# Filler products on TensorE between the attention steps of the last two groups

## The chip, the cores and the metric

The kernel runs on one core of a Trainium2 chip. The metric is the device time of one execution in microseconds (us): 2128.97 us before the change, the median of three runs (2126.75 to 2130.69). The profile is of one execution with a span of 2129.0 us, so its positions can be read against that number. Engines are named as in the profile: PE is TensorE's matrix product, PEld its weight load, DVE is VectorE, ACT is ScalarE, POOL is GpSimd, and SP issues the transfers.

## What is computed

There are 128 graphs of 128 nodes with 256 features each. Two residual layers follow one another, both on a normalised and rectified input:

```python
h = maximum(layernorm(x), 0)
x = x + gated_graph_network(h, adj, ...)      # three GRU layers
h = maximum(layernorm(x), 0)
x = x + attention(h, adj, W)

# attention
Wh = h @ W
s = Wh.sum(-1)
e = leaky_relu(s[:, :, None] + s[:, None, :], 0.2)
e = where(adj == 0, -inf, e)
alpha = softmax(e, -1)
out = alpha @ Wh
```

Everything is in float32. The change lies in the second layer, the attention, and in the layer norm ahead of it.

## The kernel before

The 128 graphs are cut into 32 groups of four (`G = 4`, `NG = 32`). Each group passes through three GRU layers and then through the attention. The work of several groups overlaps: while one group does its GRU products, earlier groups do their attention between them. At the end of the kernel this ends too. The last two groups, 30 and 31, have their attention when few or no GRU products are left, and group 31 is cut into two halves (graphs 2 and 3 first, then 0 and 1) so that one half can work while the other waits.

The order of the instructions is not that of the code. Each step calls `op(engine, ns, fn, reads, writes, ...)`, which only records a node: the engine, a cost in nanoseconds written by hand, and what it depends on. `Plan.run` then plays a schedule with these costs. It picks the engine whose earliest possible start comes first, and on this engine, among the nodes that can start at that time, the one of lowest rank. A node's rank is its due time, or that of what depends on it less the costs in between, whichever is earlier. The instructions are emitted in the order found, and each engine works them off in that order, waiting for semaphores where it must. Costs in the code are thus guesses that set the order; the chip takes the time that it takes. GRU products form a chain of fixed order.

A buffer tag has a number of instances and a kind. A write of a new instance depends on all accesses of the earlier instance that it replaces. Instances of kind "turn" are handed on in the order of their phase. `h1` has one instance, `top` and `low` two, `st`, `mv`, `rs` and `nm` eight. In PSUM there is one bank each for `x_rz`, `x_n`, `y_rz`, `y_n`, `q_rz`, `q_n`, which belong to the GRU products, and two banks `misc` for everything else.

The attention of a group, with the lines that the prediction uses:

- `normed(x1, h1)`: statistics of each graph on DVE (`st`, L488), their aggregation (`mv`, L493), the reciprocal root on POOL (`rs`, L497 and L498), a small product (`nm`, L500), and the normalised, rectified `h1` on ACT (L504).
- `hw` and `s` (L899): the row sums that the scores are made of, on DVE.
- `turn_s` (L923): four or two transposes of `s` on PE. L929, L930 and L932 make the scores `e` on DVE; L934 takes their maximum `top`, L936 makes `low` of it.
- `exps` (L941) on ACT. L943 and L944 make the sums and their reciprocals.
- In the last two groups, transposes of `e` on PE (L953) and a copy to `eT` on ACT (L955).
- `weighted` (L619): two sets of products of `h1` and `eT` on PE, each followed by a copy to `uT` on ACT (L624).
- `rows_product` (L966): the product with `W`, in two sets for four graphs. L971 on DVE scales it and adds the residual, L974 stores the result.

The GRU products of the last layer are L670. At the very start, L309 fills two banks with products of the identity matrix by itself, and L344 is a transpose of weights.

Of the kernel before, what the change touches and what calls it, by code (L numbers as in the profile page):

```python
# [36 lines left out]
class Plan:  # L37
# [25 lines left out]
        uses.append(b)  # L63
        return b

    def op(self, eng, ns, fn, reads=(), writes=(), room=(), due=None, mark=None,
           turn=None, two=False, lag=None):

        i, deps = len(self.nodes), set()
        for b in room:
            if b.prev is not None:
                deps.update(a[0] for a in b.prev.accesses)
        for is_write, group in ((False, reads), (True, writes)):
            for item in group:
                b, lo, hi = item if isinstance(item, tuple) else (item, 0, 1 << 30)
                for j, w, l, h in b.accesses:
                    if (w or is_write) and l < hi and lo < h:  # L80
                        deps.add(j)
                if is_write and b.prev is not None:
                    deps.update(a[0] for a in b.prev.accesses)
        for is_write, group in ((False, reads), (True, writes)):
            for item in group:
                b, lo, hi = item if isinstance(item, tuple) else (item, 0, 1 << 30)
                b.accesses.append((i, is_write, lo, hi))
        deps.discard(i)
        bufs = {id(x[0] if isinstance(x, tuple) else x): (x[0] if isinstance(x, tuple) else x)
                for x in list(reads) + list(writes) + list(room)}  # L90
        free = [b for b in bufs.values() if self.tags[b.tag][1] in ("free", "turn")]
        for b in free:
            b.users.append(i)
            b.left += 1
        self.nodes.append([eng, ns, fn, deps, free, self.due if due is None else due,
                           two or eng == "POOL", self.LAG[eng] if lag is None else lag])
        if due is not None:
            self.chain.append(i)
        if mark is not None:
            self.marks[mark] = i  # L100
        if turn is not None:
            self.turns.append((i, turn))
# [108 lines left out]
def kernel(  # L211
# [79 lines left out]
    def ap(b):  # L291
        return phys[(b.tag,) + b.slot]
# [187 lines left out]
        to_sbuf("ACT", D, ps, W["w1_sum"], 0)  # L480


    def normed(src, dst, lo=0, hi=G):

        st, mv, rs, nm = buf("st"), buf("mv"), buf("rs"), buf("nm")
        part = slice(lo, hi)
        for b in range(lo, hi):
            op("DVE", 415, lambda b=b: nc.vector.bn_stats(ap(st)[:, b, :], ap(src)[:, b, :]),  # L488
               [(src, b, b + 1)], [(st, b, b + 1)])

        def aggr():
            for b in range(lo, hi):
                nc.vector.bn_aggr(ap(mv)[:, b, :], ap(st)[:, b, :])  # L493
        op("DVE", 160 * (hi - lo), aggr, [st], [mv])

        def rstd():
            nc.gpsimd.tensor_tensor(ap(rs)[:, part], ap(mv)[:, part, 1], eps[:, part], OP.add)  # L497
            nc.gpsimd.tensor_tensor(ap(rs)[:, part], ap(rs)[:, part], neghalf[:, part], OP.pow)  # L498
        op("POOL", 1300, rstd, [mv], [rs])
        op("DVE", 170, lambda: nc.vector.scalar_tensor_tensor(  # L500
            ap(nm)[:, part], ap(mv)[:, part, 0], -1.0, ap(rs)[:, part], op0=OP.mult, op1=OP.mult),
           [mv, rs], [nm])
        for b in range(lo, hi):
            op("ACT", 520, lambda b=b: nc.scalar.activation(  # L504
                ap(dst)[:, b, :], ap(src)[:, b, :], AF.Relu, bias=ap(nm)[:, b:b + 1],
                scale=ap(rs)[:, b:b + 1]), [(src, b, b + 1), rs, nm], [(dst, b, b + 1)])

    def flat(b):
        return ap(b).rearrange("p q n -> p (q n)")
# [381 lines left out]
    def attention(g, a, x1, h1, lo, hi):  # L891

        part, n = slice(lo, hi), hi - lo
        w1, w1_sum = W["w1"], W["w1_sum"]
        normed(x1, h1, lo, hi)
        s = buf("s")
        for b in range(lo, hi):
            hw = buf("hw")
            op("DVE", 520, lambda b=b, hw=hw: nc.vector.scalar_tensor_tensor(  # L899
                ap(hw), ap(h1)[:, b, :], 1.0, ap(w1_sum), op0=OP.mult, op1=OP.mult,  # L900
                accum_out=ap(s)[:, b:b + 1]), [(h1, b, b + 1), w1_sum], [hw, (s, b, b + 1)],
               two=True)

        e, top, low, den, rden = (buf(t) for t in ("e", "top", "low", "den", "rden"))

        def wide(t):
            return ap(t)[:, part, None].to_broadcast([P, n, N])

        def es():
            return ap(e)[:, part]

        def small(t):
            return ap(t)[:, part]
        cost = 155 + 134 * n
        op("DVE", 150 + 66 * n, lambda: nc.vector.tensor_scalar(
            es(), ap(a)[:, part], 0.0, -BIG, op0=OP.is_equal, op1=OP.mult), [(a, lo, hi)], [e])
        s_all = buf("misc")

        def turn_s():
            for b in range(lo, hi):
                nc.tensor.transpose(flat(s_all)[:, b * N:(b + 1) * N],  # L923
                                    ap(s)[:, b:b + 1].to_broadcast([P, P]), ident)

        def spread():
            return flat(s_all)[:, lo * N:hi * N].rearrange("p (b n) -> p b n", n=N)
        op("PE", 110 * n, turn_s, [s], [s_all], [e])
        op("DVE", cost, lambda: nc.vector.tensor_tensor(es(), es(), spread(), OP.add), [s_all], [e])  # L929
        op("DVE", cost, lambda: nc.vector.tensor_tensor(es(), es(), wide(s), OP.add), [s], [e],  # L930
           two=True)
        op("DVE", cost, lambda: nc.vector.scalar_tensor_tensor(  # L932
            es(), es(), ALPHA, es(), op0=OP.mult, op1=OP.max), [], [e], two=True)
        op("DVE", cost, lambda: nc.vector.tensor_reduce(small(top), es(), AX.X, OP.max),  # L934
           [e], [top])
        op("DVE", 150, lambda: nc.vector.tensor_scalar(  # L936
            small(low), small(top), -BIG / 1e3, -1.0, op0=OP.max, op1=OP.mult), [top], [low])

        def exps():
            for b in range(lo, hi):  # L940
                nc.scalar.activation(ap(e)[:, b, :], ap(e)[:, b, :], AF.Exp, bias=ap(low)[:, b:b + 1])  # L941
        op("ACT", 320 * n, exps, [low], [e], turn=(g + 2, 1, "rz"))
        op("DVE", cost, lambda: nc.vector.tensor_reduce(small(den), es(), AX.X, OP.add), [e], [den])  # L943
        op("DVE", 170, lambda: nc.vector.reciprocal(small(rden), small(den)), [den], [rden])  # L944
        eT, uT = buf("eT"), buf("uT")
        if g < NG - 2:
            turned_weights(e, eT)
        else:
            p_e = buf("misc")

            def turn():
                for b in range(lo, hi):
                    nc.tensor.transpose(flat(p_e)[:, b * N:(b + 1) * N], ap(e)[:, b, :], ident)  # L953
            op("PE", 110 * n, turn, [e], [p_e], [eT])
            op("ACT", 190 + 100 * n, lambda: nc.scalar.copy(  # L955
                ap(eT)[:, part].rearrange("p b n -> p (b n)"), flat(p_e)[:, lo * N:hi * N]),
               [p_e], [(eT, lo, hi)])

        weighted(h1, eT, uT, lo, hi)
        for m in range(lo, hi, 2):  # L960
            ps = buf("misc")

            def rows_product(m=m, ps=ps):
                for b in range(2):
                    for k in range(KD):
                        nc.tensor.matmul(ap(ps)[:, b, :], ap(uT)[:, k, (m + b) * N:(m + b + 1) * N],  # L966
                                         ap(w1)[:, k, :], start=(k == 0), stop=(k == KD - 1))
            op("PE", 4 * 432, rows_product,
               [(uT, m // 2, m // 2 + 1), (uT, 2 + m // 2, 3 + m // 2), w1], [ps])
            for b in range(2):  # L970
                op("DVE", 480, lambda b=b, i=m + b, ps=ps: nc.vector.scalar_tensor_tensor(  # L971
                    ap(x1)[:, i, :], ap(ps)[:, b, :], ap(rden)[:, i:i + 1], ap(x1)[:, i, :],
                    op0=OP.mult, op1=OP.add), [ps, rden], [(x1, m + b, m + b + 1)])
        op("SP", 100, lambda: nc.sync.dma_start(  # L974
            out[g * G + lo:g * G + hi].rearrange("b n d -> n b d"), ap(x1)[:, part]),
           [(x1, lo, hi)], [])
# [49 lines left out]
```

## Time and profile before

| stage, us from the start | what PE does | granted clock |
|---|---|---|
| 2080 to 2090.67 | last GRU products (L670), transposes L923 of group 30 | 1.00 |
| 2090.67 to 2094.40 | L966 of group 29 | 1.00 |
| 2094.40 to 2097.00 | nothing | 0.96 |
| 2097 to 2111 | attention of group 30 | 0.52 |
| 2111 to 2114 | little: transposes L923 of group 31 | 0.97 |
| 2114 to 2121 | attention of group 31 | 0.52 |
| 2121 to 2125 | rest of group 31 | 1.00 |
| 2125 to 2129 | nothing: last L971 and the last store | 0.81 |

A stage's clock is the mean share of full TensorE speed that was granted. The profile has several views that are used below: the page with each engine's busy share and the clock in 40 slices, the chain of waits (the steps that ended last, each released by the one before it), the busy time of each engine in chosen stages, and the instructions in order of time. A count xN there is a count of instructions, not of products in the code. PE durations are modelled and overlap; the starts of the weight loads (PEld) show better how fast consecutive products run.

### The profile page before, as it was taken

How to read it: one execution, taken by the hardware profiler on the slowest of the kernel's cores; microseconds unless marked ns; L12 is line 12 of the kernel's file. 1: busy time of each engine (PE TensorE's matmuls, PEld its weight loads, DVE VectorE, ACT ScalarE, POOL GpSimd, SP SyncE). 2: the span in 40 equal slices, each digit the busy share in tenths (PEclk: the TensorE clock that was granted, in tenths of full speed). 3: DMA queues.
4: the chain of work that ended last, by engine and by line, in shares of the span. 5: the costliest groups of instructions: out<-in, count | busy, mean ns of one | idle time of the engine just before them, and what ended most of it. 6: DMA issues, size and time to landing. Idle time of an engine off the chain costs nothing. (4 is left out here: it accounts for less than half of the span.)

```text
span 2129.0 us, 34073 instructions
## 1 busy us (share of the span) xinstructions
PE 2108.4 (99%) x12550; PEld 1882.8 (88%) x12550; DVE 1701.3 (80%) x3364; ACT 1536.5 (72%) x2771; POOL 923.8 (43%) x889
## 2 busy tenths in 40 slices
PE   8999999999999999999999999999999999999997
PEld 7888888898888998889998898998889988898896
DVE  7767898778787887877888787887878887877785
ACT  5567787767777676877767777677776777676663
POOL 5544454344543435434444443444434454434331
PEclk9999999999999999999999999999999999999997
DMA  4222223232222322323222322222223222212220
GB/s 144 45 50 50 48 51 72 50 65 54 64 67 55 79 56 50 68 58 80 45 60 58 75 67 50 65 56 64 66 55 75 60 50 70 60 31 53 58 75 30
DMA packets 333430, 129.35 MB, mean 61 GB/s; under 512 B 264656, under 2 KB 333008, under 8 KB 333264
## 3 DMA queue, kind: packets, MB, share of 16 engines
q1 hardware_dynamic: 333264, 127.18, 26.3%
q8 instruction: 98, 1.61, 0.3%
q14 instruction: 68, 0.56, 0.1%
HBM read 45.36 MB, written 16.78 MB: 29 GB/s over the span
## 5 line engine op out<-in xcount | busy, mean ns | idle before, releaser
L702 ACT COPY t_rz<-y_rz 128x512 f32<-128x512 f32 x192 | 112.3, 585 | 188.8 <-PE y_rz L663 114.3
L565 POOL TENSOR_TENSOR r<-rows 128x512 f32<-128x512 f32 x128 | 140.4, 1117 | 229.8 <-ACT rows L548 99.9
L712 DVE TENSOR_TENSOR t_rz<-t_rz,q_rz 128x512 f32<-128x512 f32 x192 | 131.3, 684 | 88.0 <-PE q_rz L663 40.4
L633 POOL TENSOR_TENSOR hs<-hT 128x512 f32<-128x512 f32 x96 | 131.8, 1373 | 156.3 <-PE y_n L670 72.4
L663 PE MATMUL y_rz<-hs,s_hh 128*128 128x256 f32 x768 | 197.4, 379 | 0.3 <-ACT t_rz L702 0.3
L663 PE MATMUL y_rz<-gs,s_x 128*128 128x256 f32 x768 | 197.1, 379 | 0.0
L663 PEld LDWEIGHTS y_rz<-gs,s_x 128*128 128x128 f32 x768 | 145.9, 190 | 19.8
L637 POOL TENSOR_TENSOR hs<-hT,hs 128x256 f32<-128x256 f32 x96 | 77.0, 802 | 198.1 <-PE q_n L670 160.4
L663 PEld LDWEIGHTS y_rz<-hs,s_hh 128*128 128x128 f32 x768 | 144.0, 190 | 20.1 <-issue 1.0
L590 POOL TENSOR_TENSOR pl<-d,pl 128x512 bf16<-128x512 f32 x64 | 80.8, 1264 | 185.1 <-ACT pl L588 184.9
L568 POOL TENSOR_TENSOR p<-r 128x512 bf16<-128x512 f32 x128 | 159.6, 1267 | 0.0
L712 DVE TENSOR_TENSOR t_n<-t_n,q_n 128x512 f32<-128x512 f32 x192 | 131.3, 684 | 26.4 <-PE q_n L670 12.6
L585 POOL TENSOR_TENSOR d<-hT,pl 128x512 f32<-128x512 f32 x64 | 77.6, 1214 | 139.2 <-DVE hT L791 65.2
L608 ACT COPY aT<-misc 128x512 f32<-128x512 f32 x192 | 112.0, 585 | 27.1 <-PE misc L605 23.3
L663 PE MATMUL x_rz<-hT,s_hh 128*128 128x256 f32 x512 | 131.5, 379 | 0.0
L663 PE MATMUL x_rz<-aT,s_x 128*128 128x256 f32 x512 | 131.4, 379 | 0.0
L966 PE MATMUL misc<-w,uT 128*128 128x256 f32 x512 | 125.5, 390 | 0.8 <-ACT uT L624 0.7
L829 POOL TENSOR_TENSOR x<-x,u 128x512 f32<-128x512 f32 x64 | 82.5, 1305 | 100.1 <-DMA x<-in_x_dram 54.9
L785 DVE TENSOR_TENSOR d<-hT,u 128x512 f32<-128x512 f32 x128 | 115.4, 901 | 10.5 <-ACT u L782 10.5
L663 PE MATMUL y_n<-hs,s_hh 128*128 128x256 f32 x384 | 114.3, 379 | 0.0
L663 PE MATMUL y_n<-gs,s_x 128*128 128x256 f32 x384 | 114.3, 379 | 0.0
L966 PEld LDWEIGHTS misc<-w,uT 128*128 128x128 f32 x512 | 98.6, 196 | 15.6 <-ACT uT L624 2.1
(219 smaller groups left out, 6418.5 us busy)
## 6 DMA issues: line engine op xcount, KB each, us to landing
rows<-in_x_dram SPq DMA_DIRECT2D x32, 512.0 KB, 4.2
x<-in_x_dram SPq DMA_DIRECT2D x32, 512.0 KB, 4.0
out_dram<-x SPq DMA_DIRECT2D x31, 512.0 KB, 2.9
at<-in_adj_dram SPq DMA_DIRECT2D x32, 256.0 KB, 2.8
plT<-pl SPq DMA_TRANSPOSE x186, 3.3
rz<-in_L_gnn_w_ih_dram SPq DMA_DIRECT2D x1, 768.0 KB, 5.0
rz<-in_L_gnn_w_hh_dram SPq DMA_DIRECT2D x1, 768.0 KB, 7.7
e<-in_L_gnn_weight_dram SPq DMA_DIRECT2D x3, 256.0 KB, 7.8
```

Source lines behind the costliest of these rows:

```text
L565: op("POOL", 1106, lambda part=part: nc.gpsimd.tensor_tensor(ap(r1)[:, part], ap(rows)[:, part], top(rows)[:, part], OP.subtract), [(rows, ...
L568: op("POOL", 1050, lambda part=part: nc.gpsimd.tensor_tensor(ap(p3)[:, part], ap(r1)[:, part], top(r1)[:, part], OP.subtract), [(r1, n, n ...
L585: op("POOL", 1150, lambda k=k, r=r: nc.gpsimd.tensor_tensor(ap(r), ap(hT)[:, k], part(pl, k, 0), OP.subtract), [(hT, 2 * k, 2 * k + 2), (p ...
L590: op("POOL", 1150, lambda k=k, r=r: nc.gpsimd.tensor_tensor(part(pl, k, 2), ap(r), part(pl, k, 1), OP.subtract), [r], [(pl, k, k + 1)])
L608: op("ACT", 590, lambda k=k, ps=ps: nc.scalar.copy(ap(dst)[:, k, :], flat(ps)), [ps], [(dst, 2 * k, 2 * k + 2)])
L633: op(eng, cost, lambda: sub(ap(w)[:, 0:2, :], blocks()[:, 1::2, :], blocks()[:, 0:2, :], OP.subtract), [t], [(w, 0, 2)], two=True)
L663: nc.tensor.matmul(ap(bank)[:, half, :], ap(w)[:, i - 1, q, :], source(t, sums), start=(first and c == 0 and m == 0), stop=False, skip_gro ...
L702: op("ACT", 590, lambda: nc.scalar.copy(ap(t), ap(y)), [y], [t], mark=mark)
L712: op("DVE", 690, lambda: nc.vector.tensor_tensor(ap(t), ap(t), ap(q), OP.add), [q], [t])
L785: op("DVE", 690, lambda j=j, d=d, cols=cols: nc.vector.tensor_tensor(ap(d), ap(hT)[:, j, :], ap(u)[:, cols], OP.subtract), [(hT, lo, hi), ...
L829: op("POOL", 1290, lambda cols=cols, part=part: nc.gpsimd.tensor_tensor(part(x1), part(x1), ap(u)[:, cols], OP.add), [(u, lo, hi)], [(x1, ...
L966: nc.tensor.matmul(ap(ps)[:, b, :], ap(uT)[:, k, (m + b) * N:(m + b + 1) * N], ap(w1)[:, k, :], start=(k == 0), stop=(k == KD - 1))
```

## The change

A helper `warm(t, ns, get)` is added. It acts only in the last two groups. It records one more PE node with a planned cost of `60 + ns`: one product of the identity matrix with a small part of `t`, the result of a step that has just been recorded, and `ns // 110` products of the identity with itself. All of them accumulate into the bank `x_n`, which nobody reads any more. A filler therefore can't start before the step's result is there, nor before the last GRU step has read `x_n`. It is meant to keep PE busy while the attention's short steps run on the other engines, so that the clock is not lowered. The nodes get a due time of 10^9, so that they are taken after any real work that can start at the same time, unless something real depends on them.

Fillers are added after each graph's statistics (330), after `mv` (1100), after `nm` (440), after each graph's `h1` (440), after `top` (110) and after `low` (330 for each graph). Group 30 gets them for four graphs at once, group 31 for two graphs in each half.

```diff
-    def op(self, eng, ns, fn, reads=(), writes=(), room=(), due=None, mark=None,
+    def op(self, eng, ns, fn, reads=(), writes=(), room=(), due=None, mark=None, late=False,
            turn=None, two=False, lag=None):
...
-        self.nodes.append([eng, ns, fn, deps, free, self.due if due is None else due,
+        self.nodes.append([eng, ns, fn, deps, free, 10 ** 9 if late else self.due if due is None else due,
...
+    def warm(t, ns, get=None):
+        if plan.group < NG - 2:
+            return
+        if not after_gates:
+            phase_now, plan.phase = plan.phase, len(turns)
+            after_gates.append(buf("x_n"))
+            plan.phase = phase_now
+        b = after_gates[0]
+        def products():
+            here = flat(b)
+            what = get() if get else plain(t)[:, :P]
+            cols = what.shape[1]
+            nc.tensor.matmul(here[:, :cols], ident, what, start=False, stop=False, skip_group_check=True)
+            for _ in range(ns // 110):
+                nc.tensor.matmul(here[:, :P], ident, ident, start=False, stop=False,
+                                 skip_group_check=True)
+        op("PE", 60 + ns, products, [t, b], [], late=True)
+    after_gates = []
...
+            if dst is not src:
+                warm((st, b, b + 1), 330, lambda b=b: ap(st)[:, b, :])
...
+        if dst is not src:
+            warm(mv, 1100, lambda: ap(mv)[:, lo, :])
...
+        if dst is not src:
+            warm(nm, 440, lambda: ap(nm)[:, part])
...
         for b in range(lo, hi):
+            warm((h1, b, b + 1), 440, lambda b=b: ap(h1)[:, b, :P])
...
+        warm(top, 110, lambda: small(top))
...
+        warm(low, 330 * n, lambda: small(low))
```

## The prediction

> **What bounds the kernel now.** I read the page's shares and clock row first, then the chain of waits, then engine totals by stage over the last 41 us, then the weight loads of the same stretch in order of time. Page:
>
> ```profile
> PE 2108.4 (99%) x12550; PEld 1882.8 (88%) x12550; DVE 1701.3 (80%) x3364; ACT 1536.5 (72%) x2771; POOL 923.8 (43%) x889
> PEclk9999999999999999999999999999999999999997
> ```
>
> TensorE is busy nearly throughout, so every product added costs time unless it falls into an idle stretch. Only the last slice has a low clock. By stages:
>
> ```profile
> 2088.00:2090.67 2.67, 2.67 (x19) 2.44 (x18) 1.85 (x4) 0.93 (x2) 1.06 (x1) 1.00 0.01 3
> 2090.67:2094.40 3.73, 3.73 (x19) 2.97 (x17) 3.62 (x8) 0.91 (x2) 0.22 (x1) 1.00 0.00 0
> 2094.40:2097.00 2.60, 0.00 (x0) 0.00 (x0) 2.60 (x5) 0.89 (x4) 1.57 (x1) 0.96 0.00 0
> 2097.00:2111.00 14.00, 11.92 (x38) 9.55 (x38) 9.21 (x30) 4.28 (x9) 2.21 (x4) 0.52 0.11 37
> 2111.00:2114.00 3.00, 0.70 (x6) 0.22 (x4) 2.56 (x8) 0.46 (x2) 0.00 (x0) 0.97 0.00 0
> 2114.00:2121.00 7.00, 6.50 (x20) 5.10 (x21) 2.68 (x9) 2.31 (x7) 0.00 (x0) 0.52 0.22 75
> 2121.00:2125.00 4.00, 3.33 (x17) 2.21 (x15) 0.91 (x3) 0.74 (x2) 0.00 (x0) 1.00 0.19 66
> ```
>
> Columns are stage, length, busy us (and count) of PE, weight load, DVE, ACT and POOL, clock, DMA share, GB/s. TensorE does its last gate product until 2090.67, group 29's L966 until 2094.40, then idles 2.60 us; the next stage has clock 0.52. A second gap brings it to 0.52 again. The chain of waits goes through the slow products:
>
> ```profile
> 2098.82 2.09 PE misc L619 x8
> 2104.32 6.72 PE misc L966 x16
> 2117.76 3.42 PE misc L966 x8
> 2124.97 0.48 DVE x L971
> ```
>
> So the change aims at a real loss. Weight loads pace consecutive products; their rows give the full and half rates:
>
> ```profile
> 2077.97 0.97 PEld L619 LDWEIGHTS misc<-eT,h 128*128 128x128 f32 x8
> 2078.86 0.73 PEld L670 LDWEIGHTS y_rz<-s_hh,hs 128*128 128x128 f32 x4
> 2090.67 3.33 PEld L966 LDWEIGHTS misc<-w,uT 128*128 128x128 f32 x16
> 2098.81 1.78 PEld L619 LDWEIGHTS misc<-eT,h 128*128 128x128 f32 x8 [1.08 <-ACT eT L955]
> 1.36 1.78 PEld L309 LDWEIGHTS y_rz<-ident 128*128 128x128 f32 x8 [1.36 <-POOL ident masks.py:199]
> 3.02 1.64 PEld L309 LDWEIGHTS y_n<-ident 128*128 128x128 f32 x8
> 6.05 0.36 PEld L344 LDWEIGHTS x_rz<-ident,rz 128*128 128x128 f32 x3
> 6.37 0.36 PEld L344 LDWEIGHTS misc<-ident,rz 128*128 128x128 f32 x3
> ```
>
> L619 makes 4 float32 products of 128 columns per buffer and shows x8: **two instructions a product**. At full clock 8 of them take 2078.86-2077.97 = 0.89 us, 111 ns each, so 222 ns a product; at half clock 1.78/8 = 222 ns each. L309 is `matmul(ident, ident)`, the filler's own operation: 4 products a tile, again x8, 8 in 3.02-1.36 = 1.66 us, the half rate. Only a transpose (L344, three in 6.37-6.05 = 0.32 us) takes one instruction of 107 ns. L966's 256-column products take about 3.43 us for 16 instructions, 214 ns each.
>
> **What the Trainium skill says.** "FP8 and Floating Point Precision", TensorE Precision Notes: true FP32 goes through the array in four passes. The trace agrees: 222 ns is four times 55. "TensorE: Matmul & The Clock Gate", Part 1: the clock falls to half after an idle window of about 3.4 us and comes back after a busy one. The trace agrees on both levels (1.00 and 0.50); here a gap of 2.60 us sufficed. The same page, Part 3, what overlaps: matrix products start and end strictly in program order. The trace agrees: group 31's first L923 had its operand at 2105.77 (end of L899's second accumulator read) and ran only at 2110.67, behind the last of L966. So whatever stands behind a filler waits for all of it.
>
> **The change, part by part.** Nothing is removed. All work before about 2087.5 keeps its order, because every filler needs tile x_n, whose last reader, L815, ends at 2087.47, and TensorE is busy with gates until 2090.67.
>
> Count: a filler has 1 + ns//110 products. Group 30 (n = 4): st 4x(1+3) = 16, mv 1+10 = 11, nm 1+4 = 5, h1 4x(1+4) = 20, top 2, low 1+12 = 13: 67. Each half of group 31 (n = 2): 8+11+5+10+2+7 = 43. Together **153 products, 306 instructions**. At 111 ns that is **34.0 us** of TensorE at full clock. The planner charges 60+ns: 6.77 us for group 30 and 4.33 us for each half, 15.4 us in all. It takes a product for 110 ns, which the L344 rows show to be a transpose's price; it is half of what L309 and L619 cost.
>
> Room: the real products after 2090.67, at full clock: L966 three times 3.43 (groups 29, 30 and the two halves of 31) = 10.3, L619 32 x 0.111 = 3.55, transposes L953 and L923 16 x 0.135 = 2.16 less the four of group 30's L923, which ran earlier, = 1.62. Sum 15.5 us. From 2090.67 to the last real product's end, 2124.94, are 34.3 us, so 18.8 us of idle and half-clock time are there for fillers. By planned cost (15.4) they fit; by measured cost (34.0) they overrun by 15 us.
>
> Gain inside that sum: half-clock time returns. L619 of group 30 saves 2x0.89, its L966 about 2.9, group 31's L619 0.9, L966 about 1.3: some 7 us. I have counted it by pricing everything at full clock.
>
> Where they land: the planner takes whichever ready instruction starts first, and the lowest rank among equals. The four h1 fillers of group 30 inherit a due time, because group 31 overwrites h1 (one buffer), so they are not really late; I expect them ahead of group 29's L966. Then 4x1.11 = 4.4 us go before it; L971 on VectorE, which started at 2096.05, has to wait until about 2097.1 for the first half and 2098.8 for the second, with L832, L835 and the statistics of group 31 queued behind it: about 2 us on VectorE. Group 30's low filler (13 products, 2.9 us) goes ahead of its transposes L953, and behind them wait eT, L619, uT and L966. Between the two L619, and before each later step, more fillers stand than the gap has room for. Having been ready long before, they never wait themselves, so TensorE just runs on.
>
> Sum, assuming no idle TensorE after 2090.67 and all but two small top fillers (0.9 us) ahead of the last L966: 2090.67 + 15.5 + 33.1 = 2139.3 for its end. After it come L971 and the store, 2129.0-2124.94 = 4.06 us, as before: **2143.4**. If fillers stood last instead, TensorE alone would still run to 2140.1, so no order rescues it.
>
> Costs without a row: 20 leading products move only 2 to 6 columns. Each still loads 128 weight columns, so at most 222 ns; at least nothing. The low end takes 20x0.22 = 4.4 us off: 2139. I take the full price, since loads and products alternate at equal cost in L619. The semaphore waits of the 28 fillers cost nothing where their result is long there; at 0.05 us each (the pieces named issue in the chain of waits are 0.02 to 0.04 us) they are 1.4 us more. Buffer turnover in misc (two banks) or the longer chain through ACT could still idle TensorE for a few us: to 2150.
>
> **The rivals.** (1) **Fillers as cheap as planned**: 153x0.110 = 16.8 us fit into 18.8, the 7 us come back, and some five overruns of half a filler (0.3 us) are lost: 2129-7+1.5 = about 2123, faster. For it: the gaps and clock losses are real. Against it: x8 on L309 and L619. (2) **Partly hidden**: the small products free and half a dozen fillers behind the last L966, or gain and cost near balance: 2129 to 2138. Against it: even then 306 instructions have to finish. (3) **The clock does not stay up on identity data**, or the longer chain opens new gaps: 33 us of fillers at half rate would add far more, 2155 and up. Against it: the L309 products, made of nothing but identity, last 421 ns at the median and 274 ns at the least, so identity data had raised the clock before their row ended.
>
> **How the numbers follow.** Main case, 2138 to 2150: 0.78; (1) 0.08; (2) 0.08; (3) 0.06. Predicted 2143. The range takes in the free small products and some of (2) below, new stalls above: 2135 to 2151. Faster by over 0.2% (under 2124.7): 0.08; within: 0.03; slower: 0.89.
>
> **What would show it.** Right: weight loads of L309's kind under the new line, x306 in all, near 111 ns apart; clock 1.00 from 2090 to the end; no TensorE gap over 1 us there; first L971 after 2096 delayed; the last L966 ending near 2139. Wrong: one instruction a product, a gap left unfilled, or clock at 0.5 while fillers run.

## The result, and the profile after

With the fillers the kernel takes **2145.43 us** (median of four runs, 2145.34 to 2145.6) against 2129.24 us for the kernel before in the same comparison: 1.0077 times as long, 95% interval 1.006 to 1.0095, or some 16 us more. The clock was held as intended, and the kernel is slower all the same.

The page of the kernel after, shares, clock by slices, and the first line of the chain of waits:

```profile
PE 2130.9 (99%) x12856; PEld 1910.1 (89%) x12856; DVE 1700.8 (79%) x3364; ACT 1537.0 (72%) x2771; POOL 924.5 (43%) x889
...
PEclk9999999999999999999999999999999999999999
...
PE 98%; DVE 1%; DMA 1%; ACT 0%; issue 0%; POOL 0%; SPq 0%; DVEq 0%; POOLq 0%
```

The count of PE instructions has risen from 12550 to 12856, by **306**. The last slice's clock is up from 7 to 9 (tenths of full speed). The chain of waits of the kernel before broke off near 2096, in the waits between engines; now it runs along PE alone, back through the whole kernel, since TensorE never waits for anybody in the last stretch. Busy time by stages, columns as in the view of before:

```profile
2090.67:2094.40 3.73, 3.73 (x36) 3.73 (x35) 3.66 (x8) 0.63 (x1) 0.67 (x1) 1.00 0.00 0
2094.40:2097.00 2.60, 2.60 (x14) 2.32 (x14) 1.56 (x3) 1.28 (x4) 0.91 (x1) 1.00 0.00 0
2097.00:2111.00 14.00, 14.00 (x123) 13.87 (x123) 7.87 (x24) 3.06 (x6) 2.21 (x4) 1.00 0.11 39
2111.00:2125.00 14.00, 14.00 (x113) 13.53 (x112) 6.99 (x24) 2.54 (x7) 0.00 (x0) 1.00 0.12 39
2125.00:2139.00 14.00, 14.00 (x115) 13.64 (x114) 0.88 (x2) 1.86 (x5) 0.00 (x0) 1.00 0.06 20
```

TensorE is busy in all of every stage and the clock is 1.00 in all of them (0.80 from 2139 to the end, where no real product is slowed by it). DVE, which was busy 9.21 us from 2097 to 2111, is busy 7.87 there and 0.88 in the last stage, where it now waits for TensorE. The weight loads in order of time (start, length, line, tiles, count) say what it is doing. L499 is the leading product of a filler, L501 the identity products, L649 and L999 are the old L619 and L966 (the line numbers shift a little from kernel to kernel below):

```profile
2089.87 0.30 PEld L499 LDWEIGHTS x_n<-h,ident 128*128 128x128 f32 x2
2090.09 0.97 PEld L501 LDWEIGHTS x_n<-ident 128*128 128x128 f32 x8
...
2094.34 3.33 PEld L999 LDWEIGHTS misc<-w,uT 128*128 128x128 f32 x16
...
2098.01 2.76 PEld L501 LDWEIGHTS x_n<-ident 128*128 128x128 f32 x24
...
2137.56 1.60 PEld L999 LDWEIGHTS misc<-w,uT 128*128 128x128 f32 x8
```

Four products of the identity show x8, twelve x24. A leading product takes 2090.09-2089.87 = 0.22 us. The four h1 fillers of group 30 run from 2089.87 to 2094.34, 4.47 us, ahead of group 29's last product. The last real product ends its loads at 2139.16. VectorE's step behind group 29's L999 (L1004 is the old L971) now waits for it:

```profile
2096.38 0.87 DVE L1004 SCALAR_TENSOR_TENSOR x<-misc,rden,x 128x256 f32<-128x256 f32 x2 [1.04 <-PE misc L999]
```

Where did the 16 us go? From the end of the last gate product's loads to the end of the span it was 2129.0-2090.67 = 38.3 us before and is 2143.7-2089.87 = 53.8 us after. This stretch, called **the tail** below, is 15.5 us longer, nearly the whole difference of the medians. What comes ahead of it varies by a few us between profiles (it ended at 2089.87 in this one and at 2092.84 in one below), so profiles are compared by their tails and kernels by their medians.

### The profile page after: what moved, and what is told of

Its sections match the earlier page's. It is cut to its first block, busy times and chain, and to the rows that moved or that the text cites. A ratio compares the mean times of both kernels' runs of the same rounds, so it can differ in the third digit from the quotient of the medians.

```text
span 2143.7 us, 34689 instructions
## 1 busy us (share of the span) xinstructions
PE 2130.9 (99%) x12856; PEld 1910.1 (89%) x12856; DVE 1700.8 (79%) x3364; ACT 1537.0 (72%) x2771; POOL 924.5 (43%) x889
## 3 DMA queue, kind: packets, MB, share of 16 engines
q8 instruction: 101, 1.65, 0.3%
## 4 chain that ended last, share of the span: by engine, by line
PE 98%; DVE 1%; DMA 1%; ACT 0%; issue 0%; POOL 0%; SPq 0%; DVEq 0%; POOLq 0%
PE y_rz L693 15%; PE q_rz L693 10%; PE x_rz L693 10%; PE y_rz L700 8%; PE y_n L693 8%; PE misc L635 6%; PE q_rz L700 5%; PE x_n L693 5%; PE x_rz L700 5%; PE q_n L693 5%; PE misc L999 5%; PE y_n L700 4%; PE x_n L700 3%; PE q_n L700 3%; PE misc L649 3%; PE x_n L501 1%
## 5 line engine op out<-in xcount | busy, mean ns | idle before, releaser
L999 PE MATMUL misc<-w,uT 128*128 128x256 f32 x512 | 120.6, 380 | 0.0
L693 PEld LDWEIGHTS x_rz<-aT,s_x 128*128 128x128 f32 x512 | 97.2, 190 | 13.2
```

Of the source, the lines that this page charges most:

```text
L693: nc.tensor.matmul(ap(bank)[:, half, :], ap(w)[:, i - 1, q, :], source(t, sums), start=(first and c == 0 and m == 0), stop=False, skip_gro ...
```

## The experiments

**The theory** is the sum: after the last gate product TensorE has 15.5 us of real work at full clock, the fillers, and 4.1 us follow the last real product. As long as TensorE has no idle time in between, the tail is the sum of the three, and each product of 128 columns costs 222 ns wherever it stands. **The rivals**: the loss comes from a few places where a filler stands right ahead of a product on the chain (place); it comes only from the price that the planner was told (price); and the clock is worth nothing here, so that any filler is a loss (clock).

| kernel | fillers, us | sum, us | tail measured, us | median, us | ratio to before, 95% interval |
|---|---|---|---|---|---|
| before | 0 | | 38.3 (clock lost) | 2129.24 | |
| after | 34.0 | 53.6 | 53.8 | 2145.43 | 1.0077 (1.006 to 1.0095) |
| half the products | 18.9 | 38.5 | 38.6 | 2131.52 | 1.0009 (1.0001 to 1.0018) |
| transposes | 20.0 | 39.6 | 38.6 | 2131.06 | 1.0007 (0.9999 to 1.0016) |
| no h1 fillers in group 30 | 29.5 | 49.1 | 51.0 | 2143.78 | 1.0069 (1.0054 to 1.0084) |
| no mv fillers in group 31 | 29.1 | 48.7 | 49.3 | 2142.44 | 1.0062 (1.0047 to 1.0077) |
| identity products in bfloat16 | 13.2 | 32.8 | 33.3 | 2125.93 | 0.9984 (0.9977 to 0.9991) |
| leading products only | 6.2 | 25.8 | 37.2 (clock lost) | 2129.57 | 1.0002 (0.9993 to 1.001) |
| all bfloat16, no h1 in 30 | 7.4 | 27.0 | 32.7 | 2125.38 | 0.9981 (0.9974 to 0.9988) |
| the same, filled to plan | 12.2 | 31.8 | 33.5 | 2126.09 | 0.9985 (0.9978 to 0.9992) |
| true price in the plan | 34.0 | (see below) | 50.6 | 2143.24 | 1.0066 (1.005 to 1.0083) |
| unpaced | 7.4 | 27.0 | 33.0 | 2126.25 | 0.9986 (0.9979 to 0.9992) |

Fillers are products times 222 ns (float32), 110 ns (transpose) or 56 ns (bfloat16); the tail is that of the one profiled run of each kernel. The kernel before ran beside all of these with medians of 2129.2 to 2129.8 us.

**Half the products.**

```diff
-            for _ in range(ns // 110):
+            for _ in range(ns // 220):
```

> Same 28 fillers in the same order with the same planned costs, but ns // 220 instead of ns // 110 identity products: 85 products instead of 153. Sum theory (TensorE has no idle time after 2090, so every product costs its 222 ns): 68 x 0.222 = 15.1 us less than the changed kernel, 2130.3, or 1 to 2 us more where a filler is now too short for its gap; clock near 1.00. Place theory (the loss comes from the few fillers right ahead of a real product on the chain): about half of the loss stays, 2137. A third, that the clock is worth nothing here: 2134 or more.

Measured: 2131.52 us. 68 products fewer took 13.9 us off the median and 15.2 off the tail, 223 ns a product; TensorE is without idle time to the last product and the clock 1.00. This fits the sum, not the place theory's 2137 nor the clock theory's 2134 or more. The kernel is slower than before by some 0.1%: what the clock gives back, these fillers take.

**Transposes in place of the identity products.**

```diff
-                nc.tensor.matmul(here[:, :P], ident, ident, start=False, stop=False,
-                                 skip_group_check=True)
+                nc.tensor.transpose(here[:, :P], ident, ident)
```

> Each identity-by-identity product becomes a transpose of the identity (one instruction of 107 to 135 ns instead of two of 111 ns); the 28 leading products stay. Fillers then take 28 x 0.222 + 125 x 0.107 to 0.135 = 19.6 to 23.1 us. Sum theory: 10.9 to 14.4 us less than the changed kernel, 2131 to 2134.5, clock 1.00. Rival (transposes do not count as activity for the clock, as the Trainium skill says in TensorE: Matmul & The Clock Gate, Part 4): the clock falls to 0.5 in the stretches of transposes, real products are slow again, 2138 or more.

Measured: 2131.06 us, tail 38.6 us, at the fast end. The first stage of the tail, all filler transposes in one row (count, shortest, median and longest load in ns; the loads overlap), and three rows in order of time:

```profile
2090.60:2100.00 9.40, 9.40 (x74) 8.99 (x73) 9.03 (x17) 2.83 (x7) 1.80 (x2) 1.00 0.00 0
...
L501 PEld LDWEIGHTS x_n<-ident x125: 139/141/227, 2090.8 to 2122.9; 128*128 128x128 f32 x125
...
2108.66 1.16 PEld L501 LDWEIGHTS x_n<-ident 128*128 128x128 f32 x10
2109.79 0.30 PEld L499 LDWEIGHTS x_n<-nm,ident 128*128 128x128 f32 x2
2109.93 0.50 PEld L501 LDWEIGHTS x_n<-ident 128*128 128x128 f32 x4
```

125 instructions stand where 250 did before, and ten of them start within 2109.79-2108.66 = 1.13 us, so the planner's 110 ns is about the price of a transpose, and with it the same list of fillers in the same order is 14 us faster. The tail is 1.0 us shorter than the sum: by the starts of their loads the fillers took 19.0 us, since the small leading products take 0.14 us here instead of 0.22. The clock stays at 1.00 though some two thirds of the fillers' time is transposes. The Trainium skill ("TensorE: Matmul & The Clock Gate", Part 4) says that they do not count as activity in the same way; here they kept the clock up. From 2108.66 to 2111.94 products that are not transposes took only 0.58 us of 3.28, less than the share after which the clock fell with leading products only (below). A tail of transposes alone was not tried.

**Leave out 20 products at the most exposed place, or 22 elsewhere.**

The first kernel has no h1 fillers in group 30:

```diff
-            warm((h1, b, b + 1), 440, lambda b=b: ap(h1)[:, b, :P])
+            if g == NG - 1:
+                warm((h1, b, b + 1), 440, lambda b=b: ap(h1)[:, b, :P])
```

The second has no mv fillers in group 31:

```diff
-            warm(mv, 1100, lambda: ap(mv)[:, lo, :])
+            if plan.group == NG - 2:
+                warm(mv, 1100, lambda: ap(mv)[:, lo, :])
```

> Leaves out only group 30's four h1 fillers, 20 products that run ahead of group 29's last product L966 and hold VectorE behind it. Sum theory: 20 x 0.222 = 4.4 us less than the changed kernel, 2141.0, although VectorE's steps now come about 2 us earlier. Place theory: these four carry most of the loss, 2136 or less.

> Leaves out only group 31's two mv fillers, 22 products that stand in other places, in no one's way by the plan. Sum theory: 22 x 0.222 = 4.9 us less than the changed kernel, 2140.5. Place theory: they fill real gaps, nothing changes, 2145.

Measured: 2143.78 and 2142.44 us; tails 51.0 and 49.3 us, 2.8 and 4.5 us shorter than after the change. The place theory had the first as the large gain and the second as none; the less exposed fillers brought more. In medians the gains are 1.7 and 3.0 us, short of the 4.4 and 4.9 that the sum had forecast (2141.0 and 2140.5). In the first profile the stretch ahead of the tail is 1.0 us longer (until 2090.90) than after the change; in the second, of a run of 2143.84 us, it is 3.0 us longer, and TensorE idles for 0.48 us. The first tail falls 1.6 us short of the sum, and its weight loads show why (L987 is the old L953, L1000 the old L966):

```profile
2131.57 0.20 PEld L987 LDWEIGHTS misc<-ident,e 128*128 128x128 f32 x2 [0.21 <-ACT uT L654]
2132.01 1.59 PEld L1000 LDWEIGHTS misc<-w,uT 128*128 128x128 f32 x8 [0.25 <-ACT uT L654]
...
2134.97 0.52 PEld L649 LDWEIGHTS misc<-eT,h 128*128 128x128 f32 x4 [0.71 <-ACT uT L654]
...
2136.20 1.16 PEld L1000 LDWEIGHTS misc<-w,uT 128*128 128x128 f32 x6 [0.48 <-ACT uT L654]
```

The brackets are idle time: 0.21+0.25+0.71+0.48 = 1.65 us. The planner had used the remaining fillers earlier, none was left for the last gaps, and TensorE waited for ACT there. 4.4 less 1.65 is the 2.8 us measured.

**The identity products in bfloat16.** `ident16` is a bfloat16 copy of the identity.

```diff
-                nc.tensor.matmul(here[:, :P], ident, ident, start=False, stop=False,
+                nc.tensor.matmul(here[:, :P], ident16, ident16, start=False, stop=False,
```

> The identity-by-identity products are made in bfloat16 ([...]56 ns apart in the rows of L605 in the kernel before); the 28 leading products stay float32; order and planned costs as in the change. Fillers take 28 x 0.222 + 125 x 0.056 = 13.2 us, which fits into the 18.8 us of room. Sum theory: from the last gate product to the end 15.5 + 13.2 + 4.1 = 32.8 us plus the idle time that remains, against 38.3 before: faster than before by 3 to 5.5 us, 2124 to 2127, clock near 1.00. Rival (the clock is worth nothing, fillers only cost): no faster than before, 2129.8 or more. Rival (cheap products leave gaps and the clock falls all the same): 2129 to 2131.

Measured: 2125.93 us, **faster than before** by 3.2 us (interval 0.9977 to 0.9991), tail 33.3 us with 0.7 us idle. Group 30's product with `W`, before (L966) and here (L1001), and a filler's bfloat16 products:

```profile
2104.32 6.32 PEld L966 LDWEIGHTS misc<-w,uT 128*128 128x128 f32 x16 [0.97 <-ACT uT L624]
...
2102.60 3.32 PEld L1001 LDWEIGHTS misc<-w,uT 128*128 128x128 f32 x16 [0.49 <-DVE x L1006]
...
2106.41 0.65 PEld L503 LDWEIGHTS <-ident 128*128 128x128 bf16 x10
2107.02 0.30 PEld L501 LDWEIGHTS x_n<-nm,ident 128*128 128x128 f32 x2
```

The real product runs at full rate, and ten bfloat16 products take 0.61 us. Fillers of the same number, order and place, 125 of the 153 at a quarter of the price, turn the loss into a gain. The rival that the clock is worth nothing falls here. The kernel before bears this out without any filler: in one of the 57 runs that stood beside this kernel its granted clock was 0.999, and it took 2124.94 us; the other 56, at 0.995 to 0.998, took 2127.32 us or more.

**Leading products only, against all fillers in bfloat16.**

```diff
             nc.tensor.matmul(here[:, :cols], ident, what, start=False, stop=False, skip_group_check=True)
-            for _ in range(ns // 110):
-                nc.tensor.matmul(here[:, :P], ident, ident, start=False, stop=False,
-                                 skip_group_check=True)
```

> Only the 28 leading products (6.2 us), same order and planned costs. Real products and fillers are 21.7 us of the 34.3 us up to the last product, so TensorE must idle. If such short pulses hold the clock: 2122 to 2125. If the clock falls in the gaps as before: 2128 to 2130, since the gap of 2.6 us before the first L953 is filled by 0.2 us only.

```diff
-            nc.tensor.matmul(here[:, :cols], ident, what, start=False, stop=False, skip_group_check=True)
+            nc.tensor.matmul(here[:, :cols], ident16, what.bitcast(BF16).rearrange("p (c two) -> p c two", two=2)[:, :, 1], start=False, stop=False,
+                             skip_group_check=True)
...
-                nc.tensor.matmul(here[:, :P], ident, ident, start=False, stop=False,
+                nc.tensor.matmul(here[:, :P], ident16, ident16, start=False, stop=False,
...
-            warm((h1, b, b + 1), 440, lambda b=b: ap(h1)[:, b, :P])
+            if g == NG - 1:
+                warm((h1, b, b + 1), 440, lambda b=b: ap(h1)[:, b, :P])
```

> All filler products in bfloat16, the leading ones too (they take the upper halves of the step's result), and group 30's h1 fillers left out, so that nothing stands ahead of group 29's L966. 133 x 0.056 = 7.4 us of fillers, half of what the planner thinks. Sum theory with the clock held: floor 15.5 + 7.4 + 4.1 = 27 us, so waits on other engines set the end, 2122 to 2124. If too little filling lets the clock fall: 2126 to 2129.

Measured: 2129.57 and 2125.38 us. The second lies between its two expectations: the clock held, but 2122 to 2124 was too low. The two have nearly the same amount of fillers, 6.2 and 7.4 us, and differ in the clock. Stages of the tail, leading products only:

```profile
2094.90:2099.00 4.10, 2.39 (x16) 1.80 (x15) 4.00 (x7) 1.87 (x5) 1.10 (x1) 0.97 0.00 0
2099.00:2105.00 6.00, 6.00 (x26) 5.68 (x26) 5.29 (x20) 2.33 (x5) 2.21 (x4) 0.50 0.24 82
...
2112.50:2119.00 6.50, 6.40 (x23) 5.57 (x24) 1.17 (x5) 1.71 (x6) 0.00 (x0) 0.50 0.24 81
```

and all in bfloat16:

```profile
2094.50:2099.00 4.50, 3.51 (x50) 2.77 (x48) 4.40 (x8) 2.32 (x6) 1.57 (x1) 1.00 0.00 0
2099.00:2106.00 7.00, 6.91 (x54) 6.10 (x55) 6.83 (x25) 3.36 (x6) 2.22 (x4) 1.00 0.23 77
...
2113.00:2119.80 6.80, 6.12 (x31) 4.39 (x30) 0.89 (x3) 1.86 (x5) 0.00 (x0) 1.00 0.12 41
```

In the first, TensorE is busy for 2.39 of 4.10 us in the gap, and the next stage runs at 0.50; in the second for 3.51 of 4.50, and the clock holds. The tails differ by 37.2-32.7 = 4.5 us, 0.9 us of which are the four leading products ahead of group 29's L966 in the first. That leaves 3.6 us for the clock, if nothing else differs, and 38.3-32.7 = 5.6 us against the kernel before. A purer pair is leading products only and identity products in bfloat16: the same leading products in float32 and the same planned costs, and the second has 125 bfloat16 products more. TensorE gets some 7 us more to do, and the tail is 37.2-33.3 = 3.9 us shorter. At a tail of about 33 us TensorE's sum no longer sets the end: all in bfloat16, its loads stand idle for 5.2 us, between the steps of the other engines.

**The same, filled up to the planned time.**

```diff
-            for _ in range(ns // 110):
+            for _ in range(ns // 56):
```

> As the one before, but ns // 56 products in each filler, so that the planned cost is about the true one: 218 x 0.056 = 12.2 us of fillers. Floor 15.5 + 12.2 + 4.1 = 31.8 us against 38.3 before; clock 1.00 throughout: 2122.5 to 2124.5, the fastest of the four. If the fillers' waits or overruns cost more than thought: 2126.

Measured: 2126.09 us, tail 33.5 us. It was expected to be the fastest of its four and is not: 4.8 us more of fillers cost 0.8 us of tail. In medians the three bfloat16 kernels lie within 0.7 us of each other. Small as that is, 14 of the 18 runs with less filling are faster than the fastest of the 17 with more. Once the clock holds, more filling brings nothing.

**The same products at their true price in the plan.**

```diff
-        op("PE", 60 + ns, products, [t, b], [], late=True)
+        op("PE", 222 * (1 + ns // 110), products, [t, b], [], late=True)
```

> The same 153 float32 products, but each filler is given its measured price in the plan, 222 ns a product instead of 110. Sum theory: no order helps, since all 306 instructions have to end before the kernel does: 15.5 + 34.0 us after the last gate product, 2140 to 2143. The fillers that find no gap now stand behind the last real product, so the store of the result ends long before TensorE does. Rival (only the wrong price in the plan was at fault, a planner that knows it hides the fillers): 2123 to 2130.

Measured: 2143.24 us, tail 50.6 us. The planner now puts what finds no gap behind the last real product. Weight loads and VectorE's last row of that kernel:

```profile
2127.20 1.60 PEld L999 LDWEIGHTS misc<-w,uT 128*128 128x128 f32 x8
2128.83 0.41 PEld L499 LDWEIGHTS x_n<-nm,ident 128*128 128x128 f32 x2
...
2140.10 0.30 PEld L501 LDWEIGHTS x_n<-ident 128*128 128x128 f32 x2
...
2129.24 0.88 DVE L1004 SCALAR_TENSOR_TENSOR x<-misc,rden,x 128x256 f32<-128x256 f32 x2 [3.98 <-PE misc L999]
```

The last real product loads until 2128.80, and TensorE works on fillers until 2140.4. There is no output left to compute, but the kernel isn't over until its instructions are. Against the change that saves only the 3.2 us of tail by which the last step and the store now overlap with fillers. The last real product itself ends its loads 37.9 us into the tail, against 33.9 in the kernel before, so the fillers ahead of it did not all fit either. The price theory's 2123 to 2130 falls: the total was at fault, not the order.

**Unpaced.** As all bfloat16 without h1 in group 30, but the leading product takes the identity, and the filler waits for `x_n` only.

```diff
-        op("PE", 60 + ns, products, [t, b], [], late=True)
+        op("PE", 60 + ns, products, [b], [], late=True)
```

> The bfloat16 fillers without those of group 30's h1, as in the fast version (133 products, 7.4 us), but unpaced: the leading product takes the identity instead of the step's result, and the filler depends only on x_n being free. If pacing by results matters: fillers run as soon as they come up, real gaps stay empty at their end, the clock falls in at least one of them, 2127 to 2130. If only the amount and the place in the order matter: 2125 to 2126, as paced.

Measured: 2126.25 us (paced: 2125.38 us). The profile, of a run of 2125.23 us, has a tail of 33.0 us (paced: 32.7 us) at clock 1.00. TensorE idles at other moments there, 1.0 us ahead of the first transposes of `e` and 1.2 us ahead of a later product of `h1` and `eT`, and the clock holds. But 7 of the 20 runs took 2127.2 to 2128.6 us, five of them with a mean granted clock of 0.998; of the 54 runs of the three paced bfloat16 kernels only three took over 2127.2 us, one of them at 0.998. None of these seven has a trace, so where they lost the clock is not known. The place in the order thus gives most of the gain without the pacing by results; whether pacing makes it surer stays open.

## Why the prediction was right

- **Two instructions a product, 306 in all, 111 ns apart**: shown by the count of PE instructions (+306), the x8 and x24 of L501, and the four h1 fillers of group 30, whose 40 instructions take 4.47 us, 112 ns each. This step carried the forecast.
- **The sum**: TensorE was busy for 49.7 us from 2089.87 to 2139.56 (the last product, from 2137.67, takes 1.89 us) without a break, against 15.5 + 34.0 foreseen. That the profiled run's span of 2143.7 us meets the forecast of 2143.4 so closely is in part luck: the tail was 1.1 us longer than foreseen, and what comes ahead of it 0.8 us shorter. The median of 2145.4 us is 2 us above the forecast. The metric of that run is 1.7 us more than its span, and the span of 2129.0 us that the forecast starts from belongs to a run of 2131.72 us, not to the median.
- **Small leading products at full price**: among float32 products 222 ns for 2 to 6 columns too; the low end, that they cost nothing, is out.
- **The order by hand** held: four h1 fillers, L966 of group 29, the low filler, L953. VectorE's L832 moved from 2097.22 to 2098.51 in a run whose gates ended 0.8 us earlier, so the delay was 2.1 us, as foreseen. Wrong was the place of the two small top fillers of group 31: they stand ahead of the last L966, not behind it, and cost the 0.9 us that were taken off.
- **No order rescues it**: shown by the kernel with true prices, 2143.2 us.
- **The room and the gain**: inside the sum the 7 us came back: group 30's L966 loads in 3.33 us after the change instead of 6.32, group 31's first in 1.60 instead of 3.01, and an L619 in 0.97 instead of 1.78. As a gain of the whole kernel it is an upper end: the best bfloat16 kernel has a tail 5.6 us shorter than before, and then waits between engines set the end.
- **The rival "as cheap as planned"** was wrong about what these fillers cost, and right only in the direction of what cheap ones do (2125.9 measured in bfloat16). Its 2123 counted the 7 us twice: the room of 18.8 us already holds them, so 16.8 us of fillers in it could save at most 2.0 us. The transposes, at about the planned price, only drew level with the kernel before.

## What to carry to other kernels

Work that only keeps an engine awake must be priced by the engine's own rows, product by product: count the instructions of a like operation in the trace before trusting a planner's constant. Put the fillers' sum beside the idle time that they are to fill; past it each one adds its full length, wherever it stands. If the clock is the aim, use the cheapest operation that holds it, and stop once it holds: here bfloat16 products, a quarter of the price, turned 16 us of loss into about 3.5 us of gain.

## What the runs showed of the hardware that was not expected

- In these profiles the changes of the clock lie 3.41 us or a multiple of it apart. In the kernel before it changed at 2096.78, 2110.44, 2113.85 and 2120.68, 13.66, 3.41 and 6.83 us apart. Below are leading products only, then all bfloat16 without h1 in group 30, then unpaced; the last two are cut at whole steps back from the change after the last product (2122.29 and 2121.55). Columns are as above, with the clock third from the end:

```profile
2095.37:2098.78 3.41, 1.88 (x13) 1.58 (x14) 3.31 (x7) 1.87 (x5) 0.63 (x1) 1.00 0.00 0
2098.78:2105.60 6.82, 6.82 (x29) 6.34 (x29) 5.78 (x21) 2.93 (x6) 2.21 (x4) 0.50 0.22 77
...
2109.02:2112.43 3.41, 2.36 (x17) 1.84 (x16) 3.24 (x11) 0.99 (x3) 0.00 (x0) 1.00 0.02 5
2112.44:2119.25 6.81, 6.71 (x25) 5.79 (x25) 1.23 (x5) 1.77 (x6) 0.00 (x0) 0.50 0.23 77
...
2094.99:2098.40 3.41, 2.52 (x39) 2.09 (x37) 3.40 (x6) 1.32 (x5) 1.57 (x1) 1.00 0.00 0
...
2107.90:2111.31 3.41, 2.41 (x40) 1.92 (x37) 3.20 (x11) 1.02 (x4) 0.00 (x0) 1.00 0.45 154
```

- How much work holds the clock: after steps in which TensorE was busy for 55% and 69% (30% and 37% in the kernel before) the clock fell; after steps of 74% and 71% it held. These are few steps, and busy time, which the profile models, is a rough measure: in the second line TensorE was busy throughout, and the clock came back only after two steps. A gap need not do harm in itself: in the unpaced profile TensorE was busy for only 1.42 of the 3.10 us from 2108.90 to 2112.00, across the end of a step, and the clock held. That this decides why one and the same kernel loses the clock in some runs and not in others would fit, but is not shown.
- Among float32 products one of only 2 to 6 columns took as long as one of 128, 0.22 us. Ahead of a bfloat16 product or a transpose it took 0.14 us, where one of 128 columns took 0.22. Why is not shown.
- Transposes between float32 products did not let the clock fall: it stayed at 1.00 over a stretch of 3.28 us of which other products took 18%.
